# Graph layer with gathered rows: 71 of each step's rows fetched one by one from the SP and ACT queues, and 43 filler slots for 42

## The chip, the cores and the metric

The kernel runs on one core of a Trainium2 chip. The core has a matrix engine (PE), a vector engine (DVE), a scalar engine (ACT), a general engine (POOL) and a sync engine (SP), each with its own instruction queue, and 16 DMA engines that they share. DMAs are issued from the queues of SP, ACT and POOL; the indirect ones (a row address per partition) are issued from POOL alone in this kernel. The metric is the device time of one execution in microseconds (us). Before the change the median of three runs is 15710.4 us (15699.01 to 15711.42).

## What is computed

One layer of a graph network on 50,000 nodes of 128 numbers and 1,650,000 edges, sorted by their destination. Of the edges 50,000 are self-loops, one for each node.

```python
Xs = X[src]
m_data = Xs @ W_data.T + b_data
m_ctrl = Xs @ W_control.T + b_control
msg = jnp.where((edge_types == 0)[:, None], m_data, m_ctrl)
agg = jax.ops.segment_sum(msg, dst, num_segments=X.shape[0])
out = agg + (X @ W_self.T + b_self)
return jax.nn.relu(out)
...
x = _layernorm(x + layer(x, edge_index, edge_type_2, ...), axis=-1)
```

As the weights are the same for all edges of a type, the kernel sums the gathered rows x[src] by destination and type first, and multiplies by the weights once per node. So the bulk of the work is 1.65 million row fetches of 512 bytes and their sums.

## The kernel before

The sorted edges are cut into NBLK = 523 blocks, each of two steps (Q = 2). A step covers 12 chunks (R = 12) of 128 edges, 1536, and F = 42 edges more, the fillers. A step's destinations fall into a window of W = 60 nodes, a block's into B = 112.

**Gathers.** For each chunk `gathers` issues one indirect DMA from POOL (L428): 128 rows of x, one per partition, by a column of 128 row numbers. Six of them fill one y tile, called a pass; a block has four passes, and there are ten y tiles (SLOTS). PE waits once per pass (L435) until its six gathers have landed.

**Sums.** `products` multiplies each gathered chunk by a one-hot matrix (L447): `onehot` (L403) compares each edge's column number with 0 to 119, 60 nodes for each of two types. The products of a step add up in PSUM (`acc`): 128 numbers x 120 columns. A small product of the counts (`counts`, L411; L451) gives the number of edges per node and type, for the biases. DVE adds the step's window into the block's sums (`add`, L458), at an offset that it loads into a register.

**Fillers.** A self-loop's row is the node's own row, which the kernel has anyway (xT, loaded for L478). So in each step the first F self-loops among the 1536 places are taken out of the gathers, and the F filler edges get their places. `fill` does it on DVE (L304 to L326): it matches the running number of the self-loops with the filler numbers (L307), puts the fillers' packed row and column numbers there (L310, L314, L316 to L319), and notes which nodes' self-loops were taken out (L323, L326). These nodes' rows are added back by `left_out_*` and `begin_sums` (L471). If a step had fewer than F self-loops in its 1536 places, or a destination fell out of its window, a flag computed at the end (`find_bad`) would run a slower, general path after it.

**Column lists.** The lists hold R + 1 = 13 columns per step (R1); the thirteenth is all padding, so the one-hot and the counts are computed for 13 columns a step, and twelve are multiplied.

**The rest.** `window` (L390, L397) loads four blocks' addresses into SP's registers at once and fetches the block's own rows; `layer` (L477 to L481) multiplies the sums by the weights on PE; `moments` and `store` normalise on DVE, with a square root on ACT (L503) for every two blocks; `store_rows` (L517) writes the two blocks' rows, issued by SP. Every ten blocks SP loads the next edge lists (L159, L161), and takes the fillers through DRAM to all partitions (L289, L294).

**Order.** The program writes the order by hand: in block b the queues get window(b+3), the last add of block b-1, begin_sums(b), the one-hot of block b+2 (AHEAD = 2), then pass by pass the gathers and products with fill(b+5), layer(b-1), moments(b-1), the root and the store in between. Each engine runs its own instructions in this order and waits on semaphores where it needs another's result. `plain` blocks, the first and the last, have no fillers.

Of the kernel before, what the change touches and what calls it, by code (L numbers as in the profile page):

```python
# [2 lines left out]

# [20 lines left out]
D = 128  # L24
ROW = 4 * D
# [26 lines left out]
GB = 10  # L52
GROUPS = -(-NBLK // GB)
GC = GB * C1
AHEAD = 2
# [17 lines left out]
TBL = GROUPS * GB  # L73
# [4 lines left out]
def plain(b):  # L78

    return b == 0 or b >= NBLK - 1  # L80
# [3 lines left out]
    return bass.AP(tensor=ap.tensor, offset=ap.offset, ap=[[0, n], *ap.ap])  # L84


def straight(ctx, tc, c, x, x_t, edges_t, edges_f, dst_first, first_p, out):

# [12 lines left out]
    nc = tc.nc  # L101
# [3 lines left out]
    eds = ctx.enter_context(tc.tile_pool(name="eds", bufs=2))  # L105
# [48 lines left out]
    nc.vector.memset(stats, 0.0)  # L154
    loops = keep.tile([P, GROUPS], F32, name="loops")

    def load_edges(g):
# [219 lines left out]


    idxs = {0: idx0}
    bys, pcs, zs, pls, bases = {}, {}, {}, {}, {}  # L380
    ohs, cnts, accs, xTs, pos, hs, mvs, sds, os_ = {}, {}, {}, {}, {}, {}, {}, {}, {}

    BASES = 4
# [55 lines left out]
    def products(b, q, ks):  # L439
        y = gathers(b, ks)  # L440
        of_step = chunks_of(b, q)
        if ks[0] == of_step[0]:
            accs[b, q] = ps.tile([P, 3, W], F32, name="acc")
        acc = accs[b, q]
        for k in ks:
            r = REST_ROWS[k] if b == NBLK - 1 else SIZES[k % R]
            nc.tensor.matmul(acc[:, :2, :].rearrange("p t w -> p (t w)"), y[:r, k % PASS, :], ohs[b][:r, column(k), :],  # L447
                             start=k == of_step[0], stop=k == of_step[-1])
        if ks[-1] == of_step[-1]:
            for t in range(2):  # L450
                nc.tensor.matmul(acc[:, 2, :], to_row[:, t, :], cnts[b][:, q, t * W:(t + 1) * W],  # L451
                                 start=t == 0, stop=t == 1)
# [44 lines left out]
    def pair(b):  # L497

        return range(b // 2 * 2, b + 1) if b % 2 == 1 or b == NBLK - 1 else ()
# [6 lines left out]
    def store(bs):  # L506
        mv = mvs.pop(bs[0] // 2)
        rstd = stp.tile([B, 2], F32, name="rstd")
        nc.vector.reciprocal(rstd[:, :len(bs)], sds.pop(bs[0] // 2)[:, :len(bs)])
        for i, b in enumerate(bs):  # L510
            o = stp.tile([B, D], F32, name="o", bufs=4)
            nc.vector.tensor_scalar(o, hs.pop(b), mv[:, i, 0:1], rstd[:, i:i + 1], op0=ALU.subtract, op1=ALU.mult)  # L512
            os_[b] = o
# [5 lines left out]
    def find_bad():  # L519
# [35 lines left out]
    for b in range(1, RAHEAD):  # L555
        fill(b)
        left_out_columns(b)
        left_out_matrix(b)
        if b < AHEAD:
            onehot(b)  # L560
            counts(b)
        if b == 1:
            clear_sums()
    for b in range(NBLK + 1):
        if b == NBLK - 1:
            find_bad()
        if b + 3 < NBLK:
            window(b + 3)
        g, i = divmod(b, GB)
        if i == 0 and g + 1 < GROUPS:  # L570
            load_edges(g + 1)
        if i == 3 and g + 1 < GROUPS:
            spread_out(g + 1)
        if i == 4 and g + 1 < GROUPS:
            spread_in(g + 1)
        if b > 0:
            add(b - 1, steps_of(b - 1)[-1])
        if b < NBLK:
            begin_sums(b)
        if b + AHEAD < NBLK:  # L580
            onehot(b + AHEAD)
            counts(b + AHEAD)
        last = steps_of(b)[-1:]
        for q, (step, ks) in enumerate(passes_of(b)):
            if ks:
                products(b, step, ks)
            if q == 0 and b > 0:
                left_out_columns(b + RAHEAD - 1)
            if q == 0 and b + RAHEAD < NBLK:
                fill(b + RAHEAD)  # L590
# [243 lines left out]
@with_exitstack  # L834
def gnn_resnorm(
    ctx: ExitStack,
    tc: tile.TileContext,
    x: bass.AP,
    x_t: bass.AP,
    edges_t: bass.AP,  # L840
    edges_f: bass.AP,
    dst_first: bass.AP,
    first_p: bass.AP,
    src: bass.AP,
    dst: bass.AP,
    etype: bass.AP,
    w_data: bass.AP,
    b_data: bass.AP,
    w_ctrl: bass.AP,
    b_ctrl: bass.AP,  # L850
    w_self: bass.AP,
    b_self: bass.AP,
    out: bass.AP,
):

    nc = tc.nc  # L860
    const = ctx.enter_context(tc.tile_pool(name="const", bufs=1))

    ident = const.tile([P, P], F32, name="ident")
    make_identity(nc, ident)
    eps = const.tile([P, 1], F32, name="eps")
    nc.vector.memset(eps, EPS)
    wmsgT = const.tile([P, 2 * D], F32, name="wmsgT")
    wselfT = const.tile([P, D], F32, name="wselfT")
    w_all = const.tile([P, 3, D], F32, name="w_all")
    with tc.tile_pool(name="wts_ps", bufs=3, space=bass.MemoryType.PSUM) as wts_ps:  # L870
        for i, (w, o) in enumerate(((w_data, wmsgT[:, :D]), (w_ctrl, wmsgT[:, D:]), (w_self, wselfT))):
            w_sb = w_all[:, i, :]
            nc.scalar.dma_start(w_sb, w)
            pw = wts_ps.tile([P, D], F32, name="pw")
            nc.tensor.transpose(pw, w_sb, ident)
            nc.scalar.copy(o, pw)
    bad = const.tile([1, 1], I32, name="bad")
    c = dict(ident=ident, eps=eps, wmsgT=wmsgT, wselfT=wselfT, bad=bad,
             b_data=b_data, b_ctrl=b_ctrl, b_self=b_self)

    with ExitStack() as own:
        straight(own, tc, c, x, x_t, edges_t, edges_f, dst_first, first_p, out)
    found = nc.values_load(bad, min_val=0, max_val=4 * P,
                           skip_runtime_bounds_check_because="a count of at most 3 * P + 2")
# [51 lines left out]
```

## Time and profile before

| | |
|---|---|
| median of three runs | 15710.4 us |
| the profiled execution's own time | 15700.48 us |
| its span, from first to last instruction | 15698.7 us |
| gathers on POOL (L428) | 12,528 with idx, 21 with sdt |
| PE, products L447 | 6060.6 us busy, 25,098 of 431 ns |
| DVE, counts L411 | 3045.1 us, 523 of 5822 ns |
| DVE, one-hot L403 | 1774.8 us, 523 of 3394 ns |
| DVE, fill L307 / L310 / L314 / L323 / L326 | 1291 / 1291 / 1291 / 1284 / 2127 ns each |
| granted PE clock | 0.53 of full speed |
| read from and written to HBM | 59 GB/s over the span |

The span is the length of one profiled execution on the chip; busy time is what an engine's instructions took, and waits, register loads and the issuing of DMAs are not counted in it. [...] A matmul's mean of 431 ns overlaps with its neighbours': in the timeline twelve products take about 2.9 us.

### The profile page before, as it was taken

How to read it: one execution, taken by the hardware profiler on the slowest of the kernel's cores; microseconds unless marked ns; L12 is line 12 of the kernel's file. 1: busy time of each engine (PE TensorE's matmuls, PEld its weight loads, DVE VectorE, ACT ScalarE, POOL GpSimd, SP SyncE). 2: the span in 40 equal slices, each digit the busy share in tenths (PEclk: the TensorE clock that was granted, in tenths of full speed). 3: DMA queues.
4: the chain of work that ended last, by engine and by line, in shares of the span. 5: the costliest groups of instructions: out<-in, count | busy, mean ns of one | idle time of the engine just before them, and what ended most of it. 6: DMA issues, size and time to landing. Idle time of an engine off the chain costs nothing. (4 is left out here: it accounts for less than half of the span.)

```text
span 15698.7 us, 108076 instructions
## 1 busy us (share of the span) xinstructions
PE 7588.4 (48%) x34677; PEld 6800.0 (43%) x34678; DVE 11054.2 (70%) x13586; ACT 80.8 (1%) x268; POOL 11852.3 (75%) x12559
## 2 busy tenths in 40 slices
PE   4444444444444444444444444444444444444444
PEld 3444444444444444444444444444444444444444
DVE  8766777777776776777777776677777777667775
ACT  0000000000000000000000000000000000000000
POOL 7777777777777777777777777777777777777777
PEclk6555555555555555555555555555555555555555
DMA  2222222222222222222222222222222222222222
GB/s 63 60 59 60 60 59 60 60 59 60 59 60 60 59 60 59 60 60 59 60 60 59 60 60 59 60 59 60 59 60 60 59 60 60 59 60 60 59 60 56
DMA packets 563631, 935.70 MB, mean 60 GB/s; under 512 B 289617, under 2 KB 348580, under 8 KB 563056
## 3 DMA queue, kind: packets, MB, share of 16 engines
q0 software_dynamic: 401600, 823.20, 20.2%
q1 hardware_dynamic: 161018, 105.30, 2.5%
q8 instruction: 281, 4.60, 0.1%
q14 instruction: 294, 2.41, 0.1%
q10 hardware_dynamic: 438, 0.20, 0.0%
HBM read 897.64 MB, written 30.17 MB: 59 GB/s over the span
## 5 line engine op out<-in xcount | busy, mean ns | idle before, releaser
L428 POOL DMA_INDIRECT y<-in_x,idx x12528 | 11830.7, 944 | 3824.1 <-issue 3568.3
L447 PE MATMUL acc<-oh,y 128*128 128x120 f32 x25098 | 6060.6, 431 | 7948.3 <-PEq L435 7948.3
L447 PEld LDWEIGHTS acc<-oh,y 128*128 128x128 f32 x25098 | 5478.4, 328 | 8434.5 <-PEq L435 8424.3
L458 DVE TENSOR_TENSOR sums<-acc,sums 128x180 f32 x1046 | 354.7, 339 | 4258.6 <-PE acc L451 4256.9
L411 DVE TENSOR_REDUCE cnt<-oh 128x240 bf16<-128x3120 f32 x523 | 3045.1, 5822 | 17.8
L403 DVE TENSOR_TENSOR oh<-col,small 128x3120 f32<-128x3120 f32 x523 | 1774.8, 3394 | 0.0
L326 DVE TENSOR_REDUCE by<-old 128x84 bf16<-128x1092 f32 x521 | 1108.0, 2127 | 18.1
L307 DVE TENSOR_TENSOR m<-rk,small 128x1092 f32<-128x1092 f32 x521 | 672.9, 1291 | 17.8
L310 DVE TENSOR_TENSOR new<-m,small 128x1092 f32<-128x1092 f32 x521 | 672.8, 1291 | 17.7
L314 DVE TENSOR_REDUCE v_new<-new 128x26 f32<-128x1092 f32 x521 | 672.5, 1291 | 17.7
L323 DVE TENSOR_TENSOR old<-m,small 128x1092 f32<-128x1092 f32 x521 | 668.8, 1284 | 0.0
L481 PE MATMUL po<-wmsgT,sums 128*112 128x128 f32 x2092 | 525.5, 394 | 0.0
L481 PEld LDWEIGHTS po<-wmsgT,sums 128*112 128x112 f32 x2092 | 381.6, 252 | 109.3 <-issue 87.5
L479 PE MATMUL po<-bias,sums 3*112 3x128 f32 x1046 | 355.6, 435 | 0.0
L451 PEld LDWEIGHTS <-to_row 128*128 128x128 bf16 x2092 | 328.7, 157 | 51.3
L471 DVE TENSOR_TENSOR sums<-pl,sums 128x336 f32<-128x336 f32 x521 | 264.4, 507 | 82.0 <-DVE sums L458 44.5
L451 PE MATMUL acc<-cnt,to_row 128*128 128x60 bf16 x2092 | 321.0, 247 | 0.0
L478 PE MATMUL po<-wselfT,xT 128*112 128x128 f32 x1046 | 319.9, 408 | 0.0
L478 PEld LDWEIGHTS po<-wselfT,xT 128*112 128x112 f32 x1046 | 281.7, 318 | 0.0
L479 PEld LDWEIGHTS po<-bias,sums 3*112 3x112 f32 x1046 | 209.6, 254 | 122.6 <-issue 113.9
L477 PE MATMUL po<-ident,xT 128*112 128x128 f32 x523 | 230.5, 441 | 0.0
L341 DVE TENSOR_SCALAR z<-node_no,at 84x256 bf16<-84x256 f32 x521 | 204.2, 392 | 18.4
(115 smaller groups left out, 3184.3 us busy)
## 6 DMA issues: line engine op xcount, KB each, us to landing
y<-in_x,idx POOLq DMA_INDIRECT x12528, 2.5
xT<-in_x_t SPq DMA_DIRECT2D x523, 56.0 KB, 1.9
out<-o SPq DMA_DIRECT2D x523, 56.0 KB, 1.6
vf_all<-vd SPq DMA_DIRECT2D x53, 420.0 KB, 3.6
sdt<-in_edges_t SPq DMA_DIRECT2D x53, 390.0 KB
sdt_f<-in_edges_f SPq DMA_DIRECT2D x53, 9.8 KB
vd<-v_f SPq DMA_DIRECT2D x53, 3.3 KB
first_i<-in_dst_first SPq DMA_DIRECT2D x1, 530.0 KB
```

The source lines that it names most:

```text
L307: nc.vector.tensor_tensor(m, rk_g[g][:, i, :, None].to_broadcast([P, C1, F]), rank_no_ps[:, None, :].to_broadcast([P, C1, F]), op=ALU.is_e ...
L310: nc.vector.tensor_tensor(new.rearrange("p (q r) f -> p q r f", r=R1), m.rearrange("p (q r) f -> p q r f", r=R1), vf.rearrange("p (q f) -> ...
L314: nc.vector.tensor_reduce(v, new, AX.X, ALU.add)
L323: nc.vector.tensor_tensor(old, m, cb[:, :, None].to_broadcast([P, C1, F]), op=ALU.mult)
L326: nc.vector.tensor_reduce(by, old.rearrange("p (q r) f -> p q f r", r=R1), AX.X, ALU.add)
L403: nc.vector.tensor_tensor(oh, col_g[g][:, i, :, None].to_broadcast([P, C1, 2 * W]), num_ps[:, None, :].to_broadcast([P, C1, 2 * W]), op=AL ...
L411: nc.vector.tensor_reduce(cnt, ohs[b].rearrange("p (q r) w -> p q w r", r=R1), AX.X, ALU.add)
L428: copy = nc.gpsimd.indirect_dma_start(out=y[:r, k % PASS, :].bitcast(U8), out_offset=None, in_=x_rows, in_offset=bass.IndirectOffsetOnAxis ...
L447: nc.tensor.matmul(acc[:, :2, :].rearrange("p t w -> p (t w)"), y[:r, k % PASS, :], ohs[b][:r, column(k), :], start=k == of_step[0], stop= ...
L451: nc.tensor.matmul(acc[:, 2, :], to_row[:, t, :], cnts[b][:, q, t * W:(t + 1) * W], start=t == 0, stop=t == 1)
L478: nc.tensor.matmul(po, xT, c["wselfT"], start=True, stop=False)
L481: nc.tensor.matmul(po, a[:, t, :B], c["wmsgT"][:, t * D:(t + 1) * D], start=False, stop=t == 1)
```

## The change

Each step gets 71 edges more (S), and one filler more: 1536 + 43 + 71 = 1650 edges. The rows of the 71 are not gathered by POOL. They are fetched by plain DMAs of one row of 512 bytes each, 35 per step issued by SP and 36 by ACT (TURNS), into a tile yx of 71 partitions per step; four of these tiles are held (ROW_SLOTS). The edges' destinations and types go into the thirteenth column of the lists, so the one-hot that was computed for it is now used: one product of 71 rows per step is added to acc. The bytes at which the rows lie are row number x 512, computed by DVE for one block at a time (`offsets`, from a new list src_x that SP loads for ten blocks at once); SP and ACT load them into registers, up to 32 at a time (`single_rows`, in three parts per block, ahead by two blocks). The parts begin in lists whose halves are aligned to four numbers (BEGIN, X). The DMAs count on semaphores of their own, and PE waits for both queues' before the first such product of a block (`rows_fetched`). The first and last blocks have none of it. NBLK becomes 501.

```diff
-F = 42
+F = 43
+TURNS = (35, 36)
+S = sum(TURNS)
+LOADS = 3
+BEGIN = (0, -(-Q * TURNS[0] // 4) * 4)
+X = BEGIN[1] + -(-Q * TURNS[1] // 4) * 4
...
-BE = CE + Q * F
+BE = CE + Q * (F + S)
...
     def load_edges(g):
+        t = eds.tile([1, GB * X], I32, name="one_g")
+        nc.sync.dma_start(t, src_x[None, g * GB * X:(g + 1) * GB * X])
+        one_g[g] = t
...
+    ROW_SLOTS = AHEAD + 2
+    RANGE = dict(min_val=0, max_val=(N - 1) * ROW, skip_runtime_bounds_check_because="where a node's row is")
+    x_bytes = x.rearrange("n d -> (n d)").bitcast(U8)[None, :]
+    fetched = [[tc.alloc_semaphore(f"fetched{j}_{i}") for i in range(ROW_SLOTS)] for j in range(2)]
+
+    def offsets(b):
+
+        if not plain(b):
+            g, i = divmod(b, GB)
+            ats[b] = stp.tile([1, X], I32, name="at_x", bufs=AHEAD + 2)
+            nc.vector.tensor_scalar(ats[b], one_g[g][:, i * X:(i + 1) * X], float(ROW), None, op0=ALU.mult)
+
+    def part_of(n, part):
+
+        return min(n, 32 * part)
+
+    def single_rows(b, part):
+
+        if part == 0:
+            ys[b] = stp.tile([S, Q, D], F32, name="yx", bufs=ROW_SLOTS)
+        both = []
+        for j, (eng, dma) in enumerate(((SP, nc.sync), (ACT, nc.scalar))):
+            n = Q * TURNS[j]
+            k0, k1 = part_of(n, part), part_of(n, part + 1)
+            at = BEGIN[j]
+            _, rows = nc.values_load_multi_w_load_instructions(ats[b][0:1, at + k0:at + k1], engines=[eng], **RANGE)
+            both.append([(dma, fetched[j][b % ROW_SLOTS], *divmod(k0 + k, TURNS[j]), sum(TURNS[:j]), row)
+                         for k, row in enumerate(rows)])
+        for pair in zip_longest(*both):
+            for dma, sem, q, k, at, row in filter(None, pair):
+                copy = dma.dma_start(ys[b][at + k:at + k + 1, q, :].bitcast(U8), x_bytes[:, bass.ds(row, ROW)])
+                copy.then_inc(sem, 16)
+                tc.no_tile_sem_insts.add(copy.ins.name)
+                tc.add_to_no_dep_group(f"single{b}", copy.ins)
+
+    def rows_fetched(b):
+
+        times = len(range(b % ROW_SLOTS or ROW_SLOTS, b + 1, ROW_SLOTS))
+        for j in range(2):
+            wait = nc.tensor.wait_ge(fetched[j][b % ROW_SLOTS], 16 * Q * TURNS[j] * times)
+        tc.declare_fence(wait.ins, group=f"single{b}")
...
-                             start=k == of_step[0], stop=k == of_step[-1])
+                             start=k == of_step[0], stop=plain(b) and k == of_step[-1])
         if ks[-1] == of_step[-1]:
+            if not plain(b):
+                if q == 0:
+                    rows_fetched(b)
+                nc.tensor.matmul(acc[:, :2, :].rearrange("p t w -> p (t w)"), ys[b][:, q, :],
+                                 ohs[b][:S, q * R1 + R, :], start=False, stop=True)
...
+    for b in range(1, AHEAD + 1):
+        offsets(b)
     columns(0)
...
         if b < AHEAD:
             onehot(b)
             counts(b)
+            for part in range(LOADS):
+                single_rows(b, part)
...
             begin_sums(b)
+        offsets(b + AHEAD + 1)
         if b + AHEAD < NBLK:
...
             if q == 3 and b > 0 and pair(b - 1):
                 store(pair(b - 1))
+            if q < LOADS and not plain(b + AHEAD):
+                single_rows(b + AHEAD, q)
             if q == 3 and b > 0:
```

What is left out of the diff passes src_x along, and lays the lists out on the host: the 71 edges' destinations and types into the thirteenth column, and their sources, SP's before ACT's, into src_x.

More of the change, by code (lines that the diff above doesn't have):

```diff
@@ L2 @@
 from contextlib import ExitStack
+from itertools import zip_longest
 import concourse.bacc as bacc
@@ L84, in row_bcast, with straight @@
     return bass.AP(tensor=ap.tensor, offset=ap.offset, ap=[[0, n], *ap.ap])
-def straight(ctx, tc, c, x, x_t, edges_t, edges_f, dst_first, first_p, out):
+def straight(ctx, tc, c, x, x_t, edges_t, edges_f, src_x, dst_first, first_p, out):
     nc = tc.nc
@@ L155, in straight @@
     loops = keep.tile([P, GROUPS], F32, name="loops")
+    one_g = {}
     def load_edges(g):
+        t = eds.tile([1, GB * X], I32, name="one_g")
+        nc.sync.dma_start(t, src_x[None, g * GB * X:(g + 1) * GB * X])
+        one_g[g] = t
         t = eds.tile([P, 3, GB, C1], I32, name="sdt", bufs=1)
@@ L379, in straight @@
     idxs = {0: idx0}
-    bys, pcs, zs, pls, bases = {}, {}, {}, {}, {}
+    bys, pcs, zs, pls, bases, ats, ys = {}, {}, {}, {}, {}, {}, {}
     ohs, cnts, accs, xTs, pos, hs, mvs, sds, os_ = {}, {}, {}, {}, {}, {}, {}, {}, {}
@@ L841, in gnn_resnorm @@
     edges_f: bass.AP,
+    src_x: bass.AP,
     dst_first: bass.AP,
@@ L881, in gnn_resnorm @@
     with ExitStack() as own:
-        straight(own, tc, c, x, x_t, edges_t, edges_f, dst_first, first_p, out)
+        straight(own, tc, c, x, x_t, edges_t, edges_f, src_x, dst_first, first_p, out)
     found = nc.values_load(bad, min_val=0, max_val=4 * P,
@@ L904 @@
         rest = a[CE:].reshape(TBL - 1, BE)
-        steps = rest.reshape(TBL - 1, Q, SIZE + F)
+        steps = rest.reshape(TBL - 1, Q, SIZE + F + S)
         cols = np.full((TBL, Q, R1, P), pad, np.int32)
@@ L911 @@
             cols[NBLK - 1, :, r, :n] = rest[NBLK - 2, :CE].reshape(Q, SIZE)[:, at:at + n]
+        cols[1:NBLK - 1, :, R, :S] = steps[:NBLK - 2, :, SIZE + F:]
         fills = np.full((TBL, Q, F), pad, np.int32)
         fills[1:NBLK - 1] = steps[:NBLK - 2, :, SIZE:SIZE + F]
+        ones = np.full((TBL, X), pad, np.int32)
+        single = steps[:, :, SIZE + F:]
+        for j, n in enumerate(TURNS):
+            ones[1:, BEGIN[j]:BEGIN[j] + Q * n] = single[:, :, sum(TURNS[:j]):][:, :, :n].reshape(TBL - 1, Q * n)
         firsts = np.ascontiguousarray(cols[:, :, 0, 0])
@@ L916 @@
         fillers.append(fills.reshape(TBL * Q, F))
+        if k == "src":
+            arrays["src_x"] = ones.reshape(-1)
         if k == "dst":
@@ L929 @@
     with tile.TileContext(nc) as tc:
-        gnn_resnorm(tc, ap["x"], ap["x_t"], ap["edges_t"], ap["edges_f"], ap["dst_first"], ap["first_p"],
+        gnn_resnorm(tc, ap["x"], ap["x_t"], ap["edges_t"], ap["edges_f"], ap["src_x"], ap["dst_first"], ap["first_p"],
                     ap["src"], ap["dst"], ap["edge_type_2"],
```

## The prediction

> **What bounds the kernel now.** I read the page's busy times and costliest groups first, then the timeline of one block, then SP's waits, then the few rows that show what a DMA issue costs.
>
> ```profile
> PE 7588.4 (48%) x34677; PEld 6800.0 (43%) x34678; DVE 11054.2 (70%) x13586; ACT 80.8 (1%) x268; POOL 11852.3 (75%) x12559
> ...
> L428 POOL DMA_INDIRECT y<-in_x,idx x12528 | 11830.7, 944 | 3824.1 <-issue 3568.3
> ```
>
> POOL looks a quarter idle, but the groups put that idle time down to "issue": nothing that the profile shows was being waited for. The timeline shows it gather by gather:
>
> ```profile
> 6012.09 0.94 POOL L428 DMA_INDIRECT y<-in_x,idx  x1 [0.30 <-issue]
> 6013.34 0.94 POOL L428 DMA_INDIRECT y<-in_x,idx  x1 [0.30 <-issue]
> 6014.59 0.94 POOL L428 DMA_INDIRECT y<-in_x,idx  x1 [0.30 <-issue]
> ```
>
> A gather of 128 rows takes 0.94 us plus a fixed 0.30, one every 1.25 us. From the first gather (3.27 us) to the last (15682.19, timeline) there are 12,549 (12,528 with idx, 21 with sdt): 15678.9 / 12548 = 1.2495 us each, stalls included. So POOL is never held up: the span is 3.3 us ahead of the gathers, 12,548 periods and a tail of 16.5 us. A block of 24 gathers is 24 x 1.2495 = 29.99 us, and whatever else must happen once per block is hidden while it stays under that.
>
> SP and ACT are nearly empty:
>
> ```profile
> SPq L517 <- DVE o L512: 9464.2, 261, 57.1
> SPq L397 <- PE po L478: 5122.2, 259, 80.1
> SPq L517 <- DMA out<-o: 355.0, 264, 2.4
> ```
>
> Without the first two waits SP's own work, the third included, is 15698.7 - 9464.2 - 5122.2 = 1112 us, over 523 blocks 2.1 us a block (0.7 of it the third row). ACT is busy 80.8 us, 0.15 a block.
>
> **The change, part by part.** *Gathers removed.* Each step covers 1536 + 43 + 71 = 1650 edges instead of 1578, so the 1,650,000 edges need 2 + (1650000 - 3072) // 3300 = 501 blocks instead of 523. Block 500 holds the 228 edges left: 2 gathers. 500 x 24 + 2 = 12,002 gathers, 547 fewer: 547 x 1.2495 = 683.5 us off POOL's queue.
>
> *DVE.* F from 42 to 43 lengthens five operations per block (L307, L310, L314, L323, L326: 1291 + 1291 + 1291 + 1284 + 2124 = 7281 ns) by 1/42: 0.17 us. The one-hot and its counts (L403, L411) already had R + 1 columns per step, so they don't grow. offsets() adds one instruction over 1 x 144 numbers, between the 0.18 us of 128x26 (L318, timeline) and 0.42 of 1x530 (L190, by source line): 0.25. DVE goes from 11054.2 / 523 = 21.1 to 21.6 us of 29.99; 8.4 us cover it, and without that cover it would cost 0.4 x 500 = 210 us.
>
> *PE.* Two more fp32 products per block at 6060.6 / 25098 = 0.24 us on 14.5 us a block (7588.4 / 523): hidden. Its new wait, in the middle of a block, has the second product and the rest of the queue behind it (then DVE's add, then POOL through the ten y slots). The rows were issued two blocks earlier, and direct DMAs land in 1.6 to 3.6 us, so it costs nothing while SP and ACT keep pace.
>
> *DMA engines.* The queue summary gives SP's packets a price:
>
> ```profile
> q0 software_dynamic: 401600, 823.20, 20.2%
> q1 hardware_dynamic: 161018, 105.30, 2.5%
> ```
>
> 2.5% of 16 x 15698.7 us over 161,018 packets is 39 ns. 142 rows at two packets each (data, completion) would be 11 us a block even if all fell on one engine, beside 6 us of gathers (20.2%): under 30, hidden.
>
> *SP and ACT: the part that decides.* Per block SP issues 70 single-row DMAs and ACT 72, each with an address from a register, and three register loads each (32, 32, 6 and 32, 32, 8). No row of before is that DMA, but three stand near it:
>
> ```profile
> L149 ACTq DMA_DIRECT2D bias<-in_L_gnn_b_control x1: 232/232/232, 2.8 to 2.8; - x1
> L149 ACTq DMA_DIRECT2D bias<-in_L_gnn_b_self x1: 263/263/263, 3.1 to 3.1; - x1
> ...
> L397 SPq MOVE xT<-in_x_t x523: 29/29/29, 23.7 to 15563.2; - x175
> L397 SPq DMA_DIRECT2D xT<-in_x_t x523: 343/373/390, 23.8 to 15563.2; - x175
> ```
>
> The bias rows are one row of 512 B on one partition, exactly the new size, at a constant address: 0.232 us, and 0.263 where the instruction also waits on a semaphore; about 0.04 lies between issues (2.82 + 0.23 to 3.09). The first of the three took 0.561, which I take for a first-use cost, as the next two to other tensors are half of it. xT is a DMA with a register address: one MOVE before each (29 ns, with its gap 0.065), 128 partitions, four back to back in 1.79 us, so (1.79 - 0.38) / 3 = 0.47 each. Low bound per row: 0.232 + 0.04 + 0.065 = 0.337. High bound: 0.47. I take 0.337: the size is the bias rows', the register address adds the MOVE and shows nothing more (xT's 373 ns beside 350 for first_i, as many partitions, constant address), and the rows carry no waits but the first of a load. ACT: 72 x 0.337 = 24.3; SP: 70 x 0.337 = 23.6.
>
> ```profile
> L883 SPq TENSOR_LOAD <-bad x1: 286/286/286, 15692.2 to 15692.2; - x1
> ...
> L390 SPq TENSOR_LOAD <-base_i x131: 526/759/990, 22.9 to 15505.7; - x131
> ```
>
> One register takes 286 ns on SP (472 on ACT, same view), eight take 526 or 759. The slope is (526 - 286) / 7 = 34 ns a register, or (759 - 472) / 7 = 41, with a floor between 0.25 and 0.47; a load of 32 is then 1.35 to 1.75, and one of 6 or 8 about 0.6. With 0.1 of gaps a load, a block takes 2 x 1.55 + 0.6 + 0.3 = 4.0 us. Low bound (flat at 0.526): 1.9; high (759 per eight registers, 9 eights): 6.8 + 0.3 = 7.1.
>
> Sums: ACT 24.3 + 4.0 + 0.2 = 28.5 us a block; SP 23.6 + 4.0 + 2.1 = 29.7, against POOL's 29.99. Low ends: 26.4 and 27.6. High ends: 72 x 0.47 + 7.3 = 41.1 and 42.1. So it fits, by 0.3 us on SP. The in-order waits (xT for PE, the store for DVE's o) aren't extra: an engine with two blocks of work between two stores either arrives early and waits, or is late and no longer waits. The square root (L503), now with 144 of ACT's issues between it and the one before, holds DVE's reciprocal; late by a few us it eats the 8.4 us of cover.
>
> [...]
>
> *Start and end.* Block 500 has two gathers, so less of block 499's closing chain lies under gathers; I add 5 us, estimated from the end of the timeline, where block 521's chain from last product to store takes about that.
>
> **The rivals.**
>
> *A, POOL still paces (0.52).* 3.3 + 12001 x 1.2495 + 16.5 + 5 = 15020 us span, + 1.8 around it (15700.48 - 15698.7) = 15022. The profiled run was 9.9 below the median of the runs: **15030**. Own range 15005 to 15070.
>
> *B, SP or ACT paces, still faster (0.27).* If a row costs 0.352 (mean of the two bias rows), SP needs 24.6 + 6.1 = 30.7 and each of 500 blocks takes 0.7 longer: 15,380. For it: my margin is 0.3 us of 30. Against: its terms lean on semaphore waits the rows don't have. It spans 15,070 to 15,680.
>
> *C, the row issue on SP costs too much, slower (0.18).* Break-even is 29.99 + (15710 - 15030) / 500 = 31.35 us a block, a row at (31.35 - 6.1) / 70 = 0.361 us on SP. At 0.40 SP needs 34.1: 15030 + 500 x 4.1 = 17,080; at xT's 0.47, 39.0: 19,535. For it: the only register-addressed rows cost 0.47, and two queues issue at once all the time. Against: those rows have 112 to 128 partitions, and issue time falls with partitions (128: 373, 20: 307, 1: 232).
>
> *D, the kernel falls back on its general path (below 0.01).* The fast path needs F self-loops among the first 1536 edges of each step. Counted from the reference's inputs, the poorest step has 43 and every window stays within 60 nodes: just enough.
>
> **How the numbers follow.** About 0.2% (30 us) is what a measurement of this kernel can tell from no change; C and B meet there with 0.03. Faster is A + B = 0.79, same 0.03, slower 0.18. The time is A's. The range starts under A and reaches through B to 15,690, leaving C out.
>
> **What would show it.** 12,002 gathers at L428, still 1.25 us apart with "issue" before them: A. Gathers that wait for PE at the first of a pass, PE waiting in the middle of a block, and SP or ACT without waits for DVE o: B or C. A single-row issue of 232 ns with a 29 ns MOVE and register loads under 1.8 us confirm the sum. I'm wrong if a row costs over 0.36 us on SP, if 32 registers cost over 2.5, or if POOL's 1.25 us itself grows.

## The result, and the profile after

The changed kernel takes 15940.88 us (median of 4 runs, 15940.09 to 16005.44) against 15710.65 of the kernel before beside it: ratio 1.0156 with a 95% interval of [1.0144, 1.0168], so 1.6% or 230 us slower. The forecast was 15,030, its range ended at 15,690, and the time lies on the slower side, where rival C was. Among the experiments only e8 and e9 ran where the kernel before took its 15,700 us; for all others, on other chips or at another time, it took 17,841 to 17,983, and those are compared only with one another.

The page of the changed kernel; its profiled run is the longest of the four (16005.44). First span, busy times, the chain of waits by engine and by line, then the group of gathers:

```profile
span 16003.7 us, 254227 instructions
...
PE 6196.3 (39%) x35177; PEld 5598.3 (35%) x35178; DVE 10764.4 (67%) x13519; ACT 77.4 (0%) x257; POOL 11348.3 (71%) x12012
...
SPq 64%; issue 16%; DVE 8%; DMA 7%; PE 4%; ACTq 1%; PEld 0%; PEldq 0%; DVEq 0%; ACT 0%
SPq L457 51%; SPq L452 12%; DMA yx<-in_x 6%; DVE cnt L422 2%; DMA out<-o 1%; PE po L541 1%; DVE oh L414 1%; PE acc L508 1%; PE po L539 1%; ACTq L457 1%; SPq L408 1%; PE po L538 0%; DVE m L318 0%; DVE new L321 0%; DVE by L337 0%
...
L483 POOL DMA_INDIRECT y<-in_x,idx x12000 | 11344.9, 945 | 4577.7 <-issue 3474.2
```

The chain of the work that ended last now runs through SP's queue for 64% of the span: 51% is the issue of single rows (L457) and 12% the register loads (L452). ACT, which issues as many rows, has 1%. This group's gathers are fewer by 528 (12,528 to 12,000; with the last block's, which use another list, 12,549 to 12,002) and each is as long as before (945 ns). But POOL's idle time rose from 3824.1 to 4577.7 us, though 528 gathers fewer should have taken 528 x 0.305 = 161 us off it: some 915 us of new stalls. So POOL's account is -485.8 busy, +753.6 idle, and 37 outside the two: the 305 us between the two spans.

Who waits for whom, four of the rows (waiter, what it waited for: us in total, times, longest us):

```profile
PE acc L508 <- PEq L466: 7618.0, 486, 22.4
POOL y L483 <- issue: 3474.5, 11380, 0.3
...
POOL y L483 <- PE acc L502: 1002.4, 335, 6.4
...
DVE rstd L569 <- ACT sd L563: 116.8, 11, 17.1
```

L466 is PE's wait for the single rows, 486 times and 15.7 us on average; L508 is the product of those rows behind it. Most of that wait costs nothing, since PE is busy for 39% of the span. What costs is the third row: POOL finds its y tiles not yet multiplied, because PE stands at L466. The fourth row is small: DVE seldom waits for ACT's square root, although that root stands behind ACT's single rows.

Which queue's rows PE waits for can be read from the trace's semaphore updates. In 487 of 499 blocks the product begins right behind SP's rows, that is within 0.2 us of their last update (0.09 at the median). ACT's last row of the same block landed 55 us earlier (median; never less than 20). So it is SP's rows that are late, not ACT's. ACT's queue stands still for 1066 us in all before the root, 2.1 us a block, so its own work is 29.8 us a block (the prediction had 28.5): that is only just under POOL's 29.99.

SP's own waits, and its issues over two blocks in order of time (start, length, operation, count; the register loads aren't listed there and are the gaps):

```profile
SPq L577 <- DMA out<-o: 964.9, 252, 5.7
...
SPq L577 <- DVE o L572: 18.4, 3, 10.9
...
SPq L408 <- PE po L538: 16.4, 39, 0.6
```

```profile
7999.95 22.87 SPq L457 DMA_DIRECT2D yx<-in_x  x59
8022.98 4.05 SPq L577 DMA_DIRECT2D out<-o  x2
8028.01 0.38 SPq L408 DMA_DIRECT2D xT<-in_x_t  x1
8030.44 26.31 SPq L457 DMA_DIRECT2D yx<-in_x  x70
8056.92 0.36 SPq L408 DMA_DIRECT2D xT<-in_x_t  x1
```

Before, SP waited 9464 us for DVE's o and 5122 for PE; now 18 and 16. It never arrives early: from one xT to the next it loads, issues and stores without a pause but the wait between two stores. The one wait that grew is the second store's for the first one to land, from 355.0 to 964.9 us. The two stores of a pair are issued 4.4 us apart instead of 1.8, and from its issue to its last semaphore update a store takes 3.4 us (median) instead of 1.65.

A store has 16 such updates, and they show what it waits for. Of the first store of a pair, 15 have come after 1.60 us (median), in the kernel before after 1.61. The sixteenth comes after 4.29 us, where before it came after 1.65. So one sixteenth of the store is late and the rest is on time.

Each row and each load (duration in ns, shortest/median/longest):

```profile
L457 ACTq DMA_DIRECT2D yx<-in_x x35928: 227/228/605, 18.1 to 15926.2; - x200
L457 SPq MOVE yx<-in_x x34930: 29/29/29, 27.0 to 15978.7; - x200
L457 SPq DMA_DIRECT2D yx<-in_x x34930: 227/228/504, 27.0 to 15978.7; - x200
```

```profile
L452 ACTq TENSOR_LOAD <-at_x x1497: 718/2234/2467, 15.8 to 15922.7; - x188
L452 SPq TENSOR_LOAD <-at_x x1497: 972/2050/2318, 25.0 to 15976.0; - x188
```

A row costs what was forecast: 228 ns with a MOVE of 29, one every 0.331 us on SP. A load doesn't: SP's first of a block takes 2.05 us, its second 2.13 (32 registers each), its third, of 6, 0.98 (medians). SP's block, start to start from the trace, against the prediction's terms:

| SP, us a block | predicted | measured |
|---|---|---|
| 70 rows | 23.6 | 23.2 |
| three register loads | 4.0 | 5.3 |
| stores, their register and wait | about 1.15 (in the 2.1) | 2.45 |
| the rest | about 0.95 (in the 2.1) | 1.0 |
| sum | 29.7 | 31.9 |

31.9 is over POOL's 29.99, and over the 31.35 that the prediction named as break-even. As SP never waits for another engine, the sum must come to the time of a block (16003.7 / 501 = 31.94), so that agreement proves nothing by itself. What shows SP to pace is that it doesn't wait for the others, and that PE's products begin right behind its rows.

### The profile page after: what moved, and what is told of

Same layout as the page of the kernel before. It is cut to its first block, busy times and chain, and to the rows that moved or that the text cites. A ratio compares the mean times of both kernels' runs of the same rounds, so it can differ in the third digit from the quotient of the medians.

```text
span 16003.7 us, 254227 instructions
## 1 busy us (share of the span) xinstructions
PE 6196.3 (39%) x35177; PEld 5598.3 (35%) x35178; DVE 10764.4 (67%) x13519; ACT 77.4 (0%) x257; POOL 11348.3 (71%) x12012
## 3 DMA queue, kind: packets, MB, share of 16 engines
q10 hardware_dynamic: 72294, 18.74, 0.8%
## 4 chain that ended last, share of the span: by engine, by line
SPq 64%; issue 16%; DVE 8%; DMA 7%; PE 4%; ACTq 1%; PEld 0%; PEldq 0%; DVEq 0%; ACT 0%
SPq L457 51%; SPq L452 12%; DMA yx<-in_x 6%; DVE cnt L422 2%; DMA out<-o 1%; PE po L541 1%; DVE oh L414 1%; PE acc L508 1%; PE po L539 1%; ACTq L457 1%; SPq L408 1%; PE po L538 0%; DVE m L318 0%; DVE new L321 0%; DVE by L337 0%
## 5 line engine op out<-in xcount | busy, mean ns | idle before, releaser
L483 POOL DMA_INDIRECT y<-in_x,idx x12000 | 11344.9, 945 | 4577.7 <-issue 3474.2
L502 PEld LDWEIGHTS acc<-oh,y 128*128 128x128 f32 x24004 | 3966.6, 258 | 2131.4 <-PEq L490 2124.5
L502 PE MATMUL acc<-oh,y 128*128 128x120 f32 x24004 | 4231.3, 349 | 0.1
L508 PE MATMUL acc<-oh,yx 71*128 71x120 f32 x1996 | 581.7, 384 | 7618.1 <-PEq L466 7618.0
L508 PEld LDWEIGHTS acc<-oh,yx 71*128 71x128 f32 x1996 | 402.7, 252 | 7750.3 <-PEq L466 7750.3
L337 DVE TENSOR_REDUCE by<-old 128x86 bf16<-128x1118 f32 x499 | 1081.9, 2168 | 17.3
L321 DVE TENSOR_TENSOR new<-m,small 128x1118 f32<-128x1118 f32 x499 | 658.6, 1320 | 17.0
L318 DVE TENSOR_TENSOR m<-rk,small 128x1118 f32<-128x1118 f32 x499 | 658.6, 1320 | 17.0
L325 DVE TENSOR_REDUCE v_new<-new 128x26 f32<-128x1118 f32 x499 | 657.4, 1317 | 17.0
L334 DVE TENSOR_TENSOR old<-m,small 128x1118 f32<-128x1118 f32 x499 | 654.3, 1311 | 0.0
```

Of the source, the lines that this page charges most:

```text
L318: nc.vector.tensor_tensor(m, rk_g[g][:, i, :, None].to_broadcast([P, C1, F]), rank_no_ps[:, None, :].to_broadcast([P, C1, F]), op=ALU.is_e ...
L321: nc.vector.tensor_tensor(new.rearrange("p (q r) f -> p q r f", r=R1), m.rearrange("p (q r) f -> p q r f", r=R1), vf.rearrange("p (q f) -> ...
L325: nc.vector.tensor_reduce(v, new, AX.X, ALU.add)
L337: nc.vector.tensor_reduce(by, old.rearrange("p (q r) f -> p q f r", r=R1), AX.X, ALU.add)
L483: copy = nc.gpsimd.indirect_dma_start(out=y[:r, k % PASS, :].bitcast(U8), out_offset=None, in_=x_rows, in_offset=bass.IndirectOffsetOnAxis ...
```

## The experiments

Theory 1: SP's own sum paces the changed kernel. Theory 2, the rival: something else that grows with the rows does, whatever SP's sum is (ACT, the products' wait, the DMA engines).

| run | kernel before | this kernel | ratio, 95% interval |
|---|---|---|---|
| e9_16_16 | 15696.98 | 15392.93 | 0.9806 [0.9790, 0.9823] |
| e8_const_rows | 15696.98 | 15422.04 | 0.9825 [0.9805, 0.9844] |
| e1_no_rows | 17850.01 | 17096.69 | 0.9578 [0.9559, 0.9597] |
| e1b_no_rows | 17841.26 | 17094.82 | 0.9581 [0.9562, 0.9600] |
| r1_after_again | 17975.45 | 25509.43 | 1.4191 [1.4150, 1.4232] |
| e5_sp_rows_only | 17850.01 | 23288.58 | 1.3047 [1.3021, 1.3073] |
| e2_split_stores | 17850.01 | 24781.72 | 1.3885 [1.3862, 1.3908] |
| e2b_split_stores | 17841.26 | 24747.90 | 1.3870 [1.3847, 1.3893] |
| e2c_split_stores | 17983.15 | 25199.37 | 1.4009 [1.3985, 1.4032] |
| e2d_split_stores | 17966.54 | 25134.07 | 1.3998 [1.3975, 1.4022] |
| e4_sp31 | 17850.01 | 23613.81 | 1.3206 [1.3171, 1.3242] |
| e4b_sp31 | 17841.26 | 23566.94 | 1.3211 [1.3181, 1.3242] |
| e4c_sp31 | 17983.15 | 23762.21 | 1.3227 [1.3196, 1.3258] |
| e4d_sp31 | 17938.81 | 23781.58 | 1.3228 [1.3184, 1.3272] |
| e7_split_33 | 17841.26 | 23921.65 | 1.3403 [1.3381, 1.3425] |
| e7c_split_33 | 17983.15 | 24420.78 | 1.3584 [1.3561, 1.3607] |
| e11_32_32 | 17983.15 | 24143.84 | 1.3428 [1.3405, 1.3450] |
| e11b_32_32 | 17959.97 | 24096.81 | 1.3423 [1.3400, 1.3445] |

**Fewer rows on both queues (e9).** Sixteen rows a step each, 64 a block in all, one load of 32 registers per queue and block, 513 blocks. Not shown here, and also in e4, e7 and e11: two lines that pass over a load of no rows.

```diff
-TURNS = (35, 36)
+TURNS = (16, 16)
```

> 16 rows a step on each queue instead of 35 and 36, one register load of 32 a block, 513 blocks and 43 fillers. Theory 1: SP does 32 x 0.331 + 2.1 + 3 = 16 us a block, ACT 13, both far under POOL's 29.99: the gathers saved are all that is left, 513/523 of the time and some, 15,370 to 15,430 where the kernel before takes 15,710; where it takes 17,850, below it too, 17,400 to 17,700, as even half again of 16 us stays hidden. Theory 2 (single rows cost time in proportion to their number): 45% of the changed kernel's loss is left, no better than 15,600, or 20,000 where the kernel before takes 17,850.

Measured: 15392.93, within theory 1's range, and faster than both kernels. The page's chain and gathers, then SP's waits:

```profile
POOL 73%; issue 24%; DVE 2%; POOLq 0%; PE 0%; DMA 0%; DVEq 0%; PEldq 0%; ACT 0%; ACTq 0%
...
L485 POOL DMA_INDIRECT y<-in_x,idx x12288 | 11612.1, 945 | 3754.4 <-issue 3742.2
```

```profile
SPq L579 <- DVE o L574: 5925.9, 257, 45.6
SPq L408 <- PE po L540: 1895.6, 251, 14.4
SPq L579 <- DMA out<-o: 335.2, 258, 2.5
```

POOL has the chain again, with 12 us of idle time that isn't "issue"; SP again arrives early (5926 us for DVE, 1896 for PE). The second store's wait is back at 335 us, a store lands in 1.63 us, and a pair's issues are 1.74 apart. None of the 511 products begins right behind SP's rows. So 64 single rows a block are hidden, and what removes gathers pays: 257 gathers fewer (12,292 for 12,549) at 1.25 us are 321 us, and 304 were won.

**Rows from constant addresses (e8).** No register loads and no MOVEs; the rows fetched are others, consecutive ones.

```diff
-            _, rows = nc.values_load_multi_w_load_instructions(ats[b][0:1, at + k0:at + k1], engines=[eng], **RANGE)
+            rows = [ROW * (150 * (2 * b + j) % (N // 2) + k) for k in range(k0, k1)]
...
-                copy = dma.dma_start(ys[b][at + k:at + k + 1, q, :].bitcast(U8), x_bytes[:, bass.ds(row, ROW)])
+                copy = dma.dma_start(ys[b][at + k:at + k + 1, q, :].bitcast(U8), x_bytes[:, row:row + ROW])
```

> All 142 rows a block are fetched as in the changed kernel, but from constant places in x (other rows than the edges name): no register loads and no move before each row. Theory 1: of SP's 31.9 us a block the loads' 5.3 and the moves' 70 x 0.062 = 4.3 go, 22.3 are left, POOL paces: 15,020 to 15,080 where the kernel before takes 15,710. Theory 2 (the rows' DMAs as such, on the DMA engines, cost the time): stays at 15,800 to 15,950. Where the kernel before takes 17,850: by theory 1 far below the 25,509 of r1_after_again, as SP and ACT issue 75 instructions a block instead of 149; if the slow stretches come with the DMAs, near it.

Measured: 15422.04. Neither theory had it. Without 5.3 us of loads a block SP should have had time to spare, and the kernel should have been at 15,020 to 15,080. SP's waits and its issues:

```profile
SPq L577 <- DMA out<-o: 3846.5, 252, 20.6
SPq L577 <- DVE o L572: 31.2, 2, 19.3
```

```profile
8019.35 21.38 SPq L457 DMA_DIRECT2D yx<-in_x  x70
8040.89 17.12 SPq L577 DMA_DIRECT2D out<-o  x2
8058.16 0.38 SPq L408 DMA_DIRECT2D xT<-in_x_t  x1
8058.59 21.55 SPq L457 DMA_DIRECT2D yx<-in_x  x70
```

SP still never waits for DVE. Most of what the loads gave back went to the second store, which now stands 16 us behind the first, until that one has landed. SP's block is 21.5 us of rows, 8.2 of stores and 1.0 of the rest: 30.7, and 501 x 30.7 = 15,380. Of the first store's 16 updates 15 have come after 1.62 us (median), as in the other kernels; the sixteenth comes after 15.83. The packets show the same: in 171 of the 250 pairs seven packets of 512 bytes, a sixteenth of the store's 112, begin in one run, at the median 13.7 us after the store's issue. Ahead of them the rows' packets of both queues stand in one file: outside the 3 us behind a store's issue, 96% of them begin only when the one before has ended (98% in the changed kernel). So a sixteenth of the store takes its turn behind the rows.

How fast that file moves: in windows of 5 us the two queues issued a median of 6.2 rows a us, and 5.0 packets of 512 bytes a us began (some of them the stores'). ACT's rows began 7.2 us (median) after the end of their issue, against 0.75 in the changed kernel. There 4.6 rows a us are issued and 4.8 packets begin. So e8's rows were served at some 5 a us. At that rate the changed kernel's 142 rows would need 28 us of a block of 32, an estimate. It isn't a fixed limit: e8's rows are consecutive, and ACT's queue shows 1.3% x 16 x 15419.3 us / 72,294 = 44 ns a packet there, against 0.8% and 28 ns in the changed kernel; and in e11b, on another chip, 6.0 packets a us began (median) in those windows without a store in which 6.0 to 6.3 rows were issued. What sets the rate stays open.

**No rows at all (e1, e1b).** Rows, loads and PE's wait are left out; the product of 71 rows reads a tile of zeros, so the 71 edges are missing from the sums.

```diff
...
-            ys[b] = stp.tile([S, Q, D], F32, name="yx", bufs=ROW_SLOTS)
+            ys[b] = none
+        return
...
-                if q == 0:
-                    rows_fetched(b)
```

> Leaves out the single rows: neither SP nor ACT loads an address or fetches a row, the product reads a tile of zeros, and PE does not wait for it. All else of the change stays (501 blocks, 43 fillers, the offsets, the products). Theory 1 (SP's own queue paces the changed kernel): the removed 547 gathers are worth what was summed, POOL paces at 1.25 us a gather and the time is 15,020 to 15,070. Theory 2 (something else in the change, the longer fill, the extra products or the offsets, holds POOL or PE up): it stays above 15,200.

> The same kernel as e1_no_rows: single rows, their register loads and PE's wait for them are left out. In the first set the kernel before took 17,850 us instead of 15,710, and every queue had stretches in which a 29 ns move or a 228 ns row issue took 690 to 700 ns; so these are run again, and read beside the time of the kernel before in their own set. Where that is 15,710: theory 1 (SP's queue paces the changed kernel, the gathers are worth their sum) 15,020 to 15,070; theory 2 (something else in the change holds POOL or PE up) above 15,200. Where it is 17,850 again: 17,090 as before.

Measured: 753 and 746 us less than the kernel before beside it, where 547 gathers at 1.25 us are 683.5 (and that share of 17,850 would be 777). So DVE's longer operations and PE's extra products cost some 30 us at most, and the loss lies in the rows with their loads and PE's wait for them. The 15,020 to 15,070 forecast for a kernel before of 15,710 was not put to the test.

**The changed kernel again (r1).**

> The changed kernel itself, so that the runs of the sets before have it beside them in their own conditions. Theory 1 and 2 say nothing apart here: where the kernel before takes 15,710 it is 15,940; where that takes 17,840, it stands near or a little over the 24,750 of e2b_split_stores (theory 1: above it, as SP's queue has the wait between stores too; up to 25,700).

Measured: 25509.43 against 17975.45. On such a chip the same kernel is 42% slower than before, not 1.6%. SP's waits say that it is still SP that paces:

```profile
SPq L577 <- DMA out<-o: 308.6, 251, 2.7
...
SPq L577 <- DVE o L572: 10.2, 1, 10.2
```

It never waits for DVE. The rows themselves are longer, now and then by much:

```profile
L457 SPq MOVE yx<-in_x x34930: 1/29/1520, 31.9 to 25481.2; - x200
L457 SPq DMA_DIRECT2D yx<-in_x x34930: 1/228/1440, 33.3 to 25481.2; - x200
```

The medians are those of the changed kernel's first profile, but 10,804 of SP's instructions begin 0.6 to 0.8 us after the one ahead, 7,716 us in all; in that first profile there were 82. Why is open.

**ACT's rows left out (e5).** SP's 35 rows a step alone; ACT's 36 edges are missing from the sums.

```diff
...
+            if j == 1:
+                continue
...
-        for j in range(2):
+        for j in (0,):
             wait = nc.tensor.wait_ge(fetched[j][b % ROW_SLOTS], 16 * Q * TURNS[j] * times)
...
```

> Leaves out ACT's rows: ACT loads and fetches nothing, the product takes SP's 35 rows alone. SP's queue is as in the changed kernel. Theory 1: SP still paces; a row on SP still costs 228 ns and a load of 32 still about 2.1 us, so the time falls only by what the store's wait shrinks when half of the single rows are gone: 31.9 less 0 to 1.3 us a block, 15,280 to 15,940. [...]

Measured: 23288.58. With half of all single rows gone the kernel is still 5,400 us slower than the one before beside it. SP's waits for DVE stay at 12 us:

```profile
SPq L579 <- DVE o L574: 12.4, 2, 12.2
```

In 498 of 499 blocks the product begins right behind SP's last row, so SP paces without any of ACT's rows. Its loss of 5,439 us stands beside r1's 7,534, from another set: SP's rows alone bring most of it.

**Fewer rows on SP only (e4, four times).** 31 rows a step on SP, ACT's 36 unchanged.

```diff
-TURNS = (35, 36)
+TURNS = (31, 36)
```

> 31 rows a step on SP instead of 35, 36 on ACT as before, so 67 rows a step, 502 blocks; SP loads registers twice a block (32 and 30) instead of three times. Theory 1: SP's sum falls to 62 x 0.331 = 20.5, plus loads 4.2, plus 3.4 = 28.2 us a block, under POOL's 29.99: 502 blocks with 12,032 gathers, 15,050 to 15,110. Theory 2 (contention by rows as such, of which 6% are gone): 15,800 to 15,950.

> The same kernel as e4_sp31: 31 rows a step on SP instead of 35, stores as in the changed kernel. Where the kernel before takes 15,710: theory 1, SP at 28.2 us a block, POOL paces 502 blocks, 15,050 to 15,110; theory 2, 15,800 to 15,950. Where it takes 17,850: near 23,600 again.

> As e4_sp31, beside a kernel before that takes its usual 15,700. SP 31 rows a step, ACT's 36 unchanged. Theory 1: SP 62 x 0.331 + 2 x 2.1 + 2.45 + 1.0 = 28.2, ACT as before at 29.7, so POOL paces: 12,032 gathers, 15,060; 15,040 to 15,150. Theory 2: 15,700 or above, since only 8 of 142 rows are gone. Were ACT's sum the pace, not SP's: no change from 15,940.

> As e4c_sp31, tried again in the hope of a kernel before at 15,700. Theory 1 (SP's own sum): 15,060, between 15,040 and 15,150, since SP then needs 28.2 us a block. Theory 2 (the rows slow the kernel whatever SP's sum is) and theory 3 (ACT's sum of 29.7 with its own waits paces): 15,700 to 15,940.

Measured: 23,567 to 23,782 in four sets, always beside a kernel before of over 17,800; the forecast of 15,060 was not put to the test. Beside a kernel before near 17,950, as in r1, e4c and e4d stand 1,750 and 1,730 us below r1. Eight of 142 rows a block (and SP's short load), 6% of the rows, took off 7% of the whole time. A rival by which the time goes with the number of rows would give about that too, so the time alone decides nothing. The waits say what paces now:

```profile
DVE rstd L571 <- ACT sd L565: 10648.0, 251, 57.9
```

In e4d DVE waits 10,648 us for ACT's square root, which stands behind ACT's rows; in r1 it is 140 us. ACT's queue, which in r1 stands still for 2,178 us before the root, does so for 23 us here. Only 81 of 500 products begin right behind SP's last row (140, 112 and 336 in the other three sets; 495 of 499 in r1). So with SP relieved by eight rows a block, ACT's queue with 36 rows a step as before paces for most of the time. Whether it would beside a kernel before of 15,700, where ACT's own work is 29.8 us a block, was not seen.

**The second store moved (e2, four times).** The second store of a pair is issued after the first third of the next block's rows, so that the first has landed by then.

```diff
+    later = []
...
+            if q == 1 and later:
+                store_rows(later.pop())
...
-                for done in pair(b - 1):
-                    store_rows(done)
+                done = list(pair(b - 1))
+                for one in done[:1]:
+                    store_rows(one)
+                later += done[1:]
```

> The two output stores of a pair are no longer issued one behind the other: the second goes behind the first third of the next block's single rows on SP's queue. Theory 1: SP does about 31.9 us a block (rows 23.2, register loads 5.3, stores 2.4, the rest 1.0), of it a pair of stores lies 4.4 us apart instead of 0.5 since the second waits until the first has landed; without that wait about 1.9 us a block go, SP comes to 30.0 and the time to 15,030 to 15,150. Theory 2 (the rows themselves are late, or POOL is held up by contention): moving a store changes nothing, 15,900 to 15,980.

> The same kernel as e2_split_stores, 71 rows a step, the second store of a pair behind the first third of the next block's rows. Where the kernel before takes 15,710: theory 1, SP's 31.9 us a block less 1.9 for the wait between the stores, 15,030 to 15,150; theory 2 (rows late by contention), 15,900 to 15,980. Where it takes 17,850: far above it again, as SP's queue, with 149 instructions a block, is hit most by slow stretches.

> As e2_split_stores, beside a kernel before that takes its usual 15,700. All 71 rows stay; only the second store of a pair is issued a third of a block later, so that it no longer waits for the first to land. Theory 1: SP 31.9 less 1.25 to 1.9 us (the growth of the wait, or the whole wait of 965 us over 501 blocks) = 30.0 to 30.7 a block against POOL's 29.99: 15,040 to 15,400. If the wait for landing costs nothing of its own: 15,940 as before.

> As e2c_split_stores, tried again in the hope of a kernel before at 15,700. Theory 1: SP 31.9 less 1.25 to 1.9 us a block, 15,040 to 15,400, with no wait of the second store for the first. If that wait costs nothing of its own: 15,940.

Measured: 24,748 to 25,199, again only beside a kernel before of over 17,800. Against r1, e2c is lower by 310 us and e2d by 375. The wait of the second store in e2d:

```profile
SPq L577 <- DMA out<-o: 6.1, 4, 2.4
```

308.6 us in r1, 6.1 here: the edit takes 303 us of waiting away and the time falls by about as much. So this wait lies on the path at full length there. That the edit would take the changed kernel's 965 us away beside a kernel before of 15,700 was not seen.

**Both, and 32 rows each (e7, e11, twice each).** e7 has the store's move and TURNS = (33, 36); e11 has TURNS = (32, 32) and so no third load.

> Both repairs at once, in search of the best: stores split as in e2, 33 rows a step on SP and 36 on ACT, 501 blocks, 12,018 gathers. Theory 1: SP 66 x 0.331 = 21.9, loads 5.2, the rest 1.6, 28.7 us a block; ACT 29.7; POOL's 29.99 paces: 15,030 to 15,080 where the kernel before takes 15,710. Theory 2: above 15,700. Where the kernel before takes 17,850: above 22,000.

> As e7_split_33, beside a kernel before that takes its usual 15,700. Theory 1: SP 66 x 0.331 + 4.7 for the loads + 1.2 for two stores that no longer wait for one another + 1.0 = 28.7, so POOL paces: 12,018 gathers, 15,041; 15,020 to 15,130. Theory 2: 15,700 or above.

> Each queue carries 32 rows a step (64 a step in all, 43 fillers, 503 blocks), so the third, short load of each queue is gone too. Theory 1 (SP's own sum paces the changed kernel): SP 64 x 0.331 + 2 x 2.13 + 2.45 for the stores + 1.0 = 28.9 us a block, under POOL's 29.99, so POOL paces: 12,051 gathers x 1.2495 + 3.3 + 21.5 + 1.8 = 15,084; 15,060 to 15,120, and the stores wait for DVE again. Theory 2 (many single rows slow the kernel whatever SP's sum is, by ACT, by PE's wait for rows or by the DMA engines): 128 rows a block are 90% of 142, so the time stays at 15,700 or above.

> As e11_32_32, tried again in the hope of a kernel before at 15,700. Theory 1 (SP's sum of 28.9 us a block lies under POOL's 29.99): 15,084, between 15,060 and 15,120, with SP waiting for DVE's o again. Theory 2 (the rows slow the kernel by ACT, by PE's wait for rows or by the DMA engines, whatever SP's sum is): 15,700 or above, as 128 of 142 rows a block are still there.

Measured: e7 23,922 and 24,421, e11 24,144 and 24,097; e7c, e11 and e11b are 1,090, 1,370 and 1,410 below r1. SP doesn't wait for the others there (13 us of waits for DVE in e7c, 12 in e11b), and 486 of 499 and 496 of 501 products begin right behind its rows. The question that e11 was made for, whether the time turns sharply where SP's sum passes POOL's, stays unanswered.

## Why the prediction was wrong

*What bounded the kernel, and what the gathers are worth:* right. 12,002 gathers, 1.25 us apart at the median; e9 won 304 us of 321 by them.

*DVE, PE's products, the fall-back:* right in effect. DVE's five operations took 0.15 us a block more; a product of single rows is two matmul records, not one (1996 for 499 blocks of two), which PE's idle time hides. e1 gained 753 us, and the gathers alone are 683 to 777 by the two scales above.

*A single row, 0.337 us:* right, 0.331. The bias rows at the start of the trace were the right row to take; xT's 0.47 was rightly left as the far end. Nor did the two queues lengthen each other's issues: of SP's 34,930 row issues 26,649 overlap one of ACT's, and their median is 228 ns with and without the overlap, as is that of ACT's 35,928. In e8, with no MOVE between them, the medians are 259 and 274; what lengthens them there wasn't shown.

*The register loads, 1.55 us for 32 and 0.6 for 6:* the first step that failed, a mis-sized term. The slope of 34 to 41 ns a register was taken from the shortest load of eight (526, beside 759 and 990), or from SP's median of eight (759) beside ACT's load of one (472); SP's 759 beside SP's own 286 gives 68. The measured loads are 2.05 to 2.13 us and 0.98: from one register's 286 ns to 32 that is 57 to 59 ns each. They make 5.3 us a block for 4.0, inside the bounds given (1.9 to 7.1), but 1.3 us above the value taken.

*"The in-order waits (xT for PE, the store for DVE's o) aren't extra":* right for the two that it names, which fell to 16 and 18 us. But it left out the third row of the same list, the second store's wait for the first to land: 355 us before, booked as a fixed 0.7 a block in SP's 2.1. It isn't hidden by an SP that is late, since both ends of it are SP's own; and it isn't fixed, since a sixteenth of the store takes its turn behind the rows (its last update came after 4.29 us instead of 1.65, the other 15 on time). It became 965 us, and the stores 2.45 us a block, 1.3 more than allowed for. This is the second step that failed.

*DMA engines, "11 us a block even if all fell on one engine":* wrong, and the root of the last point. 39 ns was a packet's own busy time, a mean over SP's queue before (105.30 MB in 161,018 packets); as a rate it would be 25 packets a us. In e8 some 5 rows a us were served, which would make 28 us a block rather than 11 (an estimate). And what decides isn't whether all the packets fit into a block, but what stands in line behind them.

What stands in line can be read from the updates and the packets. A row has 2.0 semaphore updates in the changed kernel (17,262 on one semaphore for 8,680 rows) and two packets, one of 512 bytes and one of 4 (on ACT's queue 36,315 and 35,979, for 35,928 rows and the six loads at the start). The rows of both queues run in one file: outside the 3 us behind a store's issue, 98% of their packets there begin only when the one before has ended, and 96% in e8. And one of a store's 16 updates is late, in e8 with seven of its 112 packets. Why the rows go in one file, and why that sixteenth goes with them, wasn't shown; the trace doesn't say which engine a packet was on.

*The margin:* the sum was 29.7 against 29.99, so 0.3 us, with two terms of SP known to no better than several us. The two misses of 1.3 us each put it at 31.9. By its formula either alone would have left SP at about 31, in rival B, and a little faster than before. None of its signs of being wrong came (a row over 0.36 us, 32 registers over 2.5, POOL's own 1.25 grown): they watched the terms that were summed, and not SP's remaining wait. Rival C had the right side, engine and break-even, but its price was wrong: it asked for a row above 0.361 us, and the row cost 0.331.

*Shown and not shown:* that SP's queue paces the changed kernel is shown by its trace (no wait for another engine, 64% of the chain, 487 of 499 products right behind SP's rows, ACT's landed 55 us earlier) and by e9, where SP waits for the others and POOL paces. ACT isn't the cause there, but it comes next: in e4, beside a kernel before of over 17,800, it is ACT's queue that holds DVE. The sizes of the two terms are read from the trace; e8 took the loads away, and most of the time saved wasn't won, because the stores' wait grew in its place. That this wait counts at full length was seen in e2, only beside a kernel before of over 17,800. How fast the kernel would be with the second store moved, or with 62 to 66 rows on SP, stays open.

## What to carry to other kernels

When an engine with little work is filled up to just below the pace of another, list every wait of that engine in the trace of before, and ask of each whether the new work makes it longer: here SP's waits on DVE and PE shrank when SP was late (9464 us to 18, 5122 to 16), while its wait on its own DMA grew (355 us to 965), as a sixteenth of the store landed late (after 4.29 us instead of 1.65; in e8 after 15.83, behind the rows' packets). Price a stream of small DMAs by the rate at which their packets begin (some 5 rows a us in e8) and not by the busy time of a packet (39 ns here, as a rate 25 a us). And take less than the whole: 64 single rows a block gave 2% where 142 lost 1.6%.

## What was unexpected in the hardware

A load of 32 numbers into registers took 2.05 to 2.13 us on SP and 2.24 to 2.25 on ACT, 64 to 70 ns a register. Smaller loads didn't cost in proportion: SP took 0.98 us for six and 0.74 for eight (L401), ACT 0.82 for eight, and SP's load of one took 286 ns in the kernel before and 469 in the changed one.

Single rows of 512 bytes from SP and ACT were served in one file (98% of their packets in the changed kernel, outside the 3 us behind a store's issue, began only when the one before had ended). In e8, where each queue issued one every 0.30 us (median), some 5 a us were served for both together, and the first store of a pair, of 112 partitions, took 15.8 us to land instead of 1.65, for the sake of one of its 16 parts.

On seven chips the kernel before took 17,841 to 17,983 us, and in r1 and e1b, two of these sets, some queues had stretches in which instructions began about 0.7 us apart whatever they were: in r1 SP's and ACT's (10,804 and 7,835 starts 0.6 to 0.8 us after the one ahead, MOVEs of 29 ns as well as issues of 228), in e1b, without the rows, SP's (227) and PE's (767 on its own queue). So it wasn't every queue, as the expectation of e1b has it: PE's has 4 of them in r1. In r1's set the kernel before lost 14% (17,975 for 15,711) and the changed kernel, with 254,227 instructions for 108,076, 60% (25,509 for 15,941). One chip showed both: the kernel before at 17,850 in one set and at 15,697 in a later one. The cause wasn't found; the granted PE clock doesn't tell the two apart (0.51 in e9 and 0.61 in the changed kernel's first profile, 0.57 in e2c).
